# A number of fixed point rounds for each block in a graph dilation

## The chip, the cores and the metric

The kernel runs on one core of a Trainium2 chip. The metric is the device time of one execution in microseconds (us). Five engines work side by side, each with its own queue: TensorE (PE in the profile; PEld is its loading of weights), VectorE (DVE), ScalarE (ACT), GpSimd (POOL) and SyncE (SP), which here only issues transfers.

## The reference

Sixteen graphs of 1024 nodes go through four graph layers with residuals and normalizations between them. The adjacency matrices are symmetric, with about 64 neighbours in a row. The second layer first thins the graph ("dilation"), row by row, and this is the part that matters here:

```
def step(carry, n):                       # n = 0 .. 1023, in order
    row = carry[n]
    num = sum(row)
    sf = (num + 1) // 2 if num > 10 else 1
    rank = cumsum(row)
    rm = row & (rank % sf == 0)           # the middle neighbour, and the last one where num is even
    rm = rm where mask[n] != 0 and num > 1
    carry[n] = row & ~rm
    carry[:, n] = carry[:, n] & ~rm       # the same edges, seen from the other side
```

Each row takes away one or two of its edges, and since the matrix stays symmetric, what an early row takes away changes the counts and ranks of the rows after it.

## The kernel before

The kernel has two paths. `fast_kernel` computes everything under assumptions that it checks on the way. If one fails, a flag that it leaves behind is not zero, and `general_kernel`, a slower path that assumes nothing of the kind, is run after it.

The stages of the fast path follow each other: the first layer (to some 650 us), the dilation (some 650 to 1025 us), the three steps of the second layer, and layers three and four together. The dilation works on all sixteen graphs, whose patterns stay on chip as 8-bit matrices (`Y`, called `carry` in the profile). It goes through eight blocks of 128 rows (`k`), each in two groups of eight graphs (`g`): sixteen steps. A step has three parts.

- `prepare` (L1048) counts, with 64 small matmuls for each half group, the neighbours of each row and their ranks within the block (`sk`, `l1`).
- `fixed_point` (L1080) finds which edges inside the diagonal 128x128 square are removed. Every row's removal depends on how many edges the rows above it removed, so it starts from a guess (`ti`, the count if nothing were removed) and repeats a round: the threshold is made odd (`thr`, L1092), the entries whose rank meets it are marked (`mid`, L1097, 128x1024 elements), eight matmuls with a single column each add the marks of the rows above (`pd`, L1100), and the new guess is their sum with the start value (L1104). In the last two blocks each round also handles the last neighbour of a row (`even`, L1095, and eight more matmuls, L1102). The number of rounds was the constant `EVALS`. After the rounds L1107 compares the last two guesses, and an inequality goes into `bad`, which ends in the flag. The marks are taken out of the square (L1113), and the constants `negc`, `posc` and `wid` for the removals are worked out (L1117 to L1130).
- `removal` (L1133), once for each of the eight graphs, takes the block's edges out of the whole rows: ranks by eight matmuls (L1142, L1144), two ScalarE operations (`q`, L1145), a comparison with `wid` on VectorE (`keep`, L1148), an and (L1149), nine transposing matmuls (`pc`, L1152 to L1156), and a last ScalarE operation that writes the columns (L1157).

In the loop over steps the fixed point of step i is written turn by turn beside the removals of step i-1, and these in turn beside the preparation of step i+1. The first fixed point has no removals beside it; it runs beside the end of the first layer (`after`). The last removals have no fixed point beside them. A program then puts the instructions of each engine in a fixed order from this, and each engine follows its queue. The buffers in this stage: two each of `q`, `keep`, `mid`, `sk`, of the PSUM tile `s` and of the PSUM tile `pc`; one `pd`.

Of the kernel before, what the change touches and what calls it, by code (L numbers as in the profile page):

```python
# [24 lines left out]
BIG = 2.0 ** 53  # L25
LN_EPS = 1e-5
BN_EPS = 1e-5
EVALS = 6
GB = 8
QB = 4  # L30

# [608 lines left out]
def fast_kernel(ctx: ExitStack, tc: tile.TileContext, t: dict, out: bass.AP, flag: bass.AP):  # L640
# [394 lines left out]
    with ExitStack() as ph:  # L1035
# [6 lines left out]
        def words(v):  # L1042
            return v.bitcast(I32)

        def per_member(v):
            return v[:, :, None].to_broadcast([P, v.shape[1], P])
# [33 lines left out]
        def fixed_point(st, k, g):  # L1080

            ks = slice(k * P, (k + 1) * P)
            gs = slice(g * GB, (g + 1) * GB)
            st.negc = negc = tiny.tile([P, GB], F32, name="negc")
            st.wid = wid = tiny.tile([P, GB], F32, name="wid")
            v1m, l1 = st.v1m, st.l1
            nc.vector.tensor_scalar(v1m, l1, 0.5, -0.5, op0=OP.mult, op1=OP.add)
            ti = tiny.tile([P, GB], I32, name="ti")
            nc.vector.tensor_copy(ti, v1m)
            for e in range(EVALS):  # L1090
                thr = tiny.tile([P, GB], I32, name="thr")
                nc.vector.tensor_scalar(thr, ti, 1, None, op0=OP.bitwise_or)  # L1092
                if st.with_last:
                    even = tiny.tile([P, GB], BF16, name="even")
                    nc.vector.tensor_tensor(even, thr, ti, op=OP.is_equal)  # L1095
                mid = sb.tile([P, GB, P], FP8, name="mid")
                nc.vector.tensor_tensor(mid, st.sk, per_member(thr), op=OP.is_equal, saturate=False)  # L1097
                pd = ps_d.tile([P, GB], F32, name="pd")
                for i in range(GB):
                    nc.tensor.matmul(pd[:, i:i + 1], mid[:, i, :], onec, start=True, stop=not st.with_last)  # L1100
                    if st.with_last:
                        nc.tensor.matmul(pd[:, i:i + 1], st.last[:, i, :], even[:, i:i + 1], start=False, stop=True)  # L1102
                tn = tiny.tile([P, GB], I32, name="ti")
                nc.vector.tensor_tensor(tn, pd, v1m, op=OP.add)  # L1104
                prev, ti = ti, tn
                yield
            nc.vector.tensor_tensor(bad[:, 0, k, gs], ti, prev, op=OP.not_equal)  # L1107
            if st.with_last:
                nc.vector.tensor_tensor(st.last, st.last, per_member(even), op=OP.mult, saturate=False)
                nc.vector.tensor_tensor(words(mid), words(mid), words(st.last), op=OP.bitwise_or)  # L1110
            for q in range(GB // QB):
                yw = words(Yq[g * GB // QB + q][:, :, k, ks])
                nc.vector.tensor_tensor(yw, yw, words(mid[:, q * QB:(q + 1) * QB]), op=OP.bitwise_xor)  # L1113


            v = tiny.tile([P, GB], F32, name="v")
            nc.vector.tensor_sub(v, l1, ti)  # L1117
            hw = tiny.tile([P, GB], F32, name="hw")
            nc.vector.tensor_tensor(hw, thr, prev, op=OP.is_equal)
            nc.vector.tensor_sub(negc, hw, v)  # L1120
            nc.vector.scalar_tensor_tensor(hw, v, 0.5, hw, op0=OP.mult, op1=OP.mult)
            nc.vector.tensor_sub(negc, negc, hw)
            st.posc = posc = tiny.tile([P, GB], F32, name="posc")
            nc.vector.scalar_tensor_tensor(posc, v, 2.0, negc, op0=OP.mult, op1=OP.add)
            en = tiny.tile([P, GB], F32, name="en")
            mk = mok[:, g * GB * NT + k:(g + 1) * GB * NT:NT]
            nc.vector.scalar_tensor_tensor(en, v, 10.5, mk, op0=OP.is_gt, op1=OP.mult)
            nc.vector.tensor_tensor(bad[:, 1, k, gs], en, mk, op=OP.not_equal)
            nc.vector.scalar_tensor_tensor(hw, hw, 1.0, en, op0=OP.add, op1=OP.mult)
            nc.vector.tensor_scalar(wid, hw, -1.0, None, op0=OP.add)  # L1130
            yield
# [40 lines left out]
        G2 = B // GB  # L1172
        steps = [(Batch(), k, g) for k in range(NT) for g in range(G2)]
        in_rounds([chain(*(prepare(*s) for s in steps[:G2]), fixed_point(*steps[0])), after(state[B - 1], B - 1)])
        ending.close()
        ps_c = ph.enter_context(tc.tile_pool(name="dl_pc", bufs=2, space=PSUM, reuse_waits="tile"))
# [13 lines left out]
        for i in range(1, len(steps) + 1):  # L1190
            streams = [fixed_point(*steps[i])] if i < len(steps) else []
            streams.append(removals(steps[i - 1], steps[i - 1 + G2] if i - 1 + G2 < len(steps) else None))
            take_turns(streams)
# [672 lines left out]
```

## Time and profile before

| what | us |
|---|---|
| median of three runs (lowest, highest) | 2735.02 (2731.83, 2736.03) |
| the profiled execution | 2734.11 |
| its span | 2732.4 |
| first round of the dilation starts (L1089) | 649.5 |
| first `q` of the removals | 672.4 |
| last L1157 of the dilation ends | 1024.9 |

The profile is a record of one execution. A busy share counts the time in which an engine has an instruction under way. Successive VectorE operations overlap a little: an operation of 1.22 us holds the engine some 1.14 us. "Idle before" is the time for which an engine had nothing under way ahead of an instruction, with the instruction on another engine that ended the wait. In the timeline each line has its start, its duration, the engine and line, what it writes and reads, and the shapes.

From the first `q` of one step to that of the next, the steps of the dilation take (us): 21.4, 22.1, 21.1, 21.0, 21.0, 20.9, 20.9, 20.9, 20.9, 20.9, 21.6, 23.4, 28.0, 22.7, 24.7.

### The profile page before, as it was taken

The numbers are of one execution on the slowest core, as the hardware profiler recorded it, in microseconds if no ns is written. First come the engines' busy times: TensorE is split into PE (matmuls) and PEld (weight loads), VectorE is DVE, ScalarE is ACT, GpSimd is POOL, SyncE is SP. The second block draws the span as 40 slices with busy tenths as digits, with TensorE's granted clock in tenths as the row PEclk, the third lists the DMA queues.
The fourth block names the chain that finished last, engine by engine and source line by source line (L and its number), as shares of the span: only waits on it lengthen the run. The fifth ranks groups of instructions, "written<-read, shape, count | busy, mean of one in ns | idle before, by whom it ended". The sixth has DMA issues, their size and how long they took to land.

```text
span 2732.4 us, 41821 instructions
## 1 busy us (share of the span) xinstructions
PE 2552.2 (93%) x15048; PEld 1688.8 (62%) x15048; DVE 2108.6 (77%) x5650; ACT 1977.0 (72%) x3188; POOL 317.1 (12%) x287
## 2 busy tenths in 40 slices
PE   7999999994899888998999998999999999999986
PEld 3444444442666657887778887456666666666655
DVE  5887778875999986776678877577787787787785
ACT  6888889873888786666655543777777777777773
POOL 0000000003000001121112123001010010001001
PEclk9999999996999999999999999999999999999998
DMA  5455445430000042233356655101222211111100
GB/s 189 162 169 171 165 167 177 157 114 23 2 2 2 2 183 96 94 108 124 132 203 224 254 205 211 39 24 62 70 77 73 90 62 62 62 62 62 46 24 25
DMA packets 120810, 285.38 MB, mean 104 GB/s; under 512 B 12305, under 2 KB 65425, under 8 KB 113425
## 3 DMA queue, kind: packets, MB, share of 16 engines
q1 hardware_dynamic: 101280, 203.33, 22.4%
q0 software_dynamic: 19312, 79.28, 7.5%
q8 instruction: 121, 1.98, 0.3%
q14 instruction: 97, 0.79, 0.1%
HBM read 202.72 MB, written 79.82 MB: 103 GB/s over the span
## 4 chain that ended last, share of the span: by engine, by line
PE 62%; DVE 16%; issue 9%; POOL 5%; ACT 4%; DMA 3%; SPq 0%; POOLq 0%; ACTq 0%; DVEq 0%
PE acc L974 8%; PE ph L1618 8%; PE pmm L724 8%; PE acc L1678 7%; PE ph L766 6%; PE acc L1306 5%; PE ph L759 4%; PE pmm L1690 3%; POOL rn L745 2%; PE ph L1605 2%; PE ph L1432 2%; DVE mid L1097 2%; POOL ln_rstd L745 1%; PE s L1144 1%; DVE keep L1148 1%
## 5 line engine op out<-in xcount | busy, mean ns | idle before, releaser
L745 POOL TENSOR_TENSOR ln_rstd<-ln_rstd,mhalf 128x8 f32<-128x8 f32 (+1 forms) x68 | 108.3, 1592 | 1347.6 <-DVE ln_rstd L742 879.7
L974 PE MATMUL acc<-em,hs 128*128 128x512 f32 x512 | 260.1, 607 | 1.9 <-DVE past L1075 1.3
L724 PE MATMUL pmm<-xT,G 128*128 128x512 f32 x512 | 261.8, 604 | 0.0
L1678 PE MATMUL acc<-ex,hs 128*128 128x512 f32 x512 | 248.9, 596 | 7.4 <-DVE hs L1705 4.5
L801 ACT ACTIVATE xn<-xn,ln_nb,ln_rstd 128x128 f32<-128x128 f32 x512 | 204.6, 481 | 70.3 <-DVE ln_nb L799 70.3
L1306 PE MATMUL acc<-a,lo 128*128 128x512 f32 x768 | 240.4, 398 | 15.3 <-DVE lo L1273 15.3
L1306 PE MATMUL acc<-a,hi 128*128 128x512 f32 x768 | 241.4, 399 | 3.8 <-ACT hi L1272 3.6
L986 ACT ACTIVATE em<-em,mx 128x1024 f32<-128x1024 f32 x128 | 146.4, 1144 | 63.5 <-DVE mx L984 63.0
L1698 ACT ACTIVATE ex<-em,mn 128x1024 f32<-128x1024 f32 x128 | 146.8, 1147 | 44.6 <-DVE mn L1695 43.9
L984 DVE CUSTOM_DVE_ANT_0 em<-pmm,msk 128x1024 f32<-128x1024 f32 x128 | 156.0, 1219 | 27.0 <-PE pmm L724 26.4
L1306 PEld LDWEIGHTS acc<-a,lo 128*128 128x128 f32 x768 | 144.3, 190 | 52.2 <-DVE lo L1273 22.6
L1690 PE MATMUL pmm<-G,hT 128*128 128x512 f32 (+3 forms) x416 | 175.3, 523 | 0.1
L1695 DVE CUSTOM_DVE_ANT_0 em<-pmm,msk 128x1024 f32<-128x1024 f32 x128 | 155.3, 1214 | 24.4 <-PE pmm L1692 22.3
L1306 PEld LDWEIGHTS acc<-a,hi 128*128 128x128 f32 x768 | 144.1, 191 | 34.1 <-ACT hi L1272 4.6
L1157 ACT ACTIVATE carry<-pc,negone 128x1024 fp8e4<-128x1024 f32 x128 | 140.8, 1114 | 27.0 <-PE pc L1156 21.7
L932 ACT ACTIVATE carry<-an 128x1024 fp8e4<-128x1024 f32 x128 | 134.4, 1050 | 21.7 <-DMA an<-in_adj 20.7
L981 ACT ACTIVATE msk<-carry,l0nbig 128x1024 bf16<-128x1024 fp8e4 x128 | 145.4, 1137 | 0.0
L1618 PE MATMUL ph<-A,hi 128*128 128x512 f32 x512 | 143.1, 420 | 1.2 <-DVE zn L1607 0.7
L1686 ACT ACTIVATE msk<-A,nbig 128x1024 bf16<-128x1024 fp8e4 x128 | 144.1, 1136 | 0.0
L1678 PEld LDWEIGHTS acc<-ex,hs 128*128 128x128 f32 x512 | 88.7, 190 | 76.8 <-issue 54.6
L1295 ACT CAST a<-A 128x1024 fp32r<-128x1024 fp8e4 x96 | 99.1, 1050 | 50.9 <-PE acc L1306 50.9
L1295 ACT CAST a<-carry 128x1024 fp32r<-128x1024 fp8e4 x96 | 99.3, 1049 | 47.6 <-PE acc L1306 47.4
(319 smaller groups left out, 6237.4 us busy)
## 6 DMA issues: line engine op xcount, KB each, us to landing
an<-in_adj SPq DMA_DIRECT2D x128, 512.0 KB, 3.6
adj_d<-carry POOLq DMA_DIRECT2D x16, 1024.0 KB, 4.2
A<-dil_d SPq DMA_DIRECT2D x16, 1024.0 KB, 5.6
rdeg<-rdeg_d SPq DMA_DIRECT2D x32, 512.0 KB, 3.8
A<-adj_d SPq DMA_DIRECT2D x16, 1024.0 KB, 4.8
ag_d<-ag POOLq DMA_DIRECT2D x24, 512.0 KB, 5.0
ag<-ag_d SPq DMA_DIRECT2D x24, 512.0 KB, 5.0
xn<-in_x SPq DMA_DIRECT2D x16, 512.0 KB, 4.3
```

The lines of the kernel that those rows point to most:

```text
L724: nc.tensor.matmul(p[:, h * 512:(h + 1) * 512], lhsT, rhs[:, h * 512:(h + 1) * 512], start=True, stop=True)
L745: nc.gpsimd.tensor_tensor(r, r, mhalf[:, :n], op=OP.pow)
L766: nc.tensor.matmul(p, W, x[:, c], start=(i == 0), stop=(i == len(pairs) - 1))
L801: nc.scalar.activation(r[:, k.start + i, :], r[:, k.start + i, :], AF.Identity, scale=rstd[:, i:i + 1], bias=nb[:, i:i + 1])
L974: nc.tensor.matmul(s.acc[:, c], hs, em[:, c], start=(jt == 0), stop=(jt == NT - 1))
L984: nc.vector.tensor_tensor_reduce(em, e, msk, 1.0, 3.0e38, op0=OP.add, op1=OP.min, accum_out=mn)
L1295: nc.scalar.copy(a, A[:, 2 * i:2 * i + 2, c])
L1306: nc.tensor.matmul(acc, part[:, jt, :], pieces[h * NT // 2 + i][:, j, :], start=(jt == 0 and p == 0), stop=(jt == NT - 1 and p == 1))
L1618: nc.tensor.matmul(p, part[:, jt, :], A[jt][:, c], start=(jt == 0 and i == 0), stop=(jt == NT - 1 and i == 1))
L1678: nc.tensor.matmul(s.acc[:, c], hs, ex[:, c], start=(jt == 0), stop=(jt == NT - 1))
L1690: nc.tensor.matmul(e[:, c], s.hT[:, js], s.G[:, c], start=True, stop=True)
L1695: nc.vector.tensor_tensor_reduce(row, e, msk, 1.0, 0.0, op0=OP.add, op1=OP.min, accum_out=mn)
```

## The change

The constant becomes a tuple with an entry for each block, and the loop takes the entry of its block. The comparison of the last two guesses and the flag stay, so a block that isn't settled after its rounds still sends the whole computation through the general path.

```
-EVALS = 6
+EVALS = 2, 3, 4, 7, 7, 3, 3, 9
...
             nc.vector.tensor_copy(ti, v1m)
-            for e in range(EVALS):
+            for e in range(EVALS[k]):
                 thr = tiny.tile([P, GB], I32, name="thr")
                 nc.vector.tensor_scalar(thr, ti, 1, None, op0=OP.bitwise_or)
```

Blocks 0, 1, 2, 5 and 6 get fewer rounds, blocks 3, 4 and 7 more.

## The prediction

> **What bounds the kernel now.** I read the page's engine shares first. TensorE is busy 93% of the span, but the change touches only one stage, so what it is worth has to be read there. The stage was found with the groups by line (L1097, the comparison inside the loop that changes, runs only between 649 and 1002 us), and then cut into stretches.
>
> ```profile
> span 2732.4 us, 41821 instructions
> PE 2552.2 (93%) x15048; PEld 1688.8 (62%) x15048; DVE 2108.6 (77%) x5650; ACT 1977.0 (72%) x3188; POOL 317.1 (12%) x287
> ```
>
> The view of busy time by stretches. The first is the fixed point of the first block alone, the next three are single steps of the steady part, the fifth is the step with the last fixed point, the sixth is the last removals alone:
>
> ```profile
> 649.00:672.00 23.00, 10.82 (x147) 7.54 (x146) 20.14 (x73) 3.36 (x9) 1.64 (x1) 0.50 0.03 10
> 737.00:758.00 21.00, 18.95 (x254) 13.46 (x251) 20.13 (x58) 18.23 (x25) 0.00 (x0) 1.00 0.01 2
> 758.00:779.00 21.00, 19.00 (x254) 13.61 (x251) 20.11 (x57) 18.24 (x26) 0.00 (x0) 1.00 0.01 2
> 779.00:800.00 21.00, 19.03 (x254) 13.62 (x252) 20.10 (x57) 18.27 (x26) 0.00 (x0) 1.00 0.01 2
> 979.30:1004.00 24.70, 18.19 (x255) 13.46 (x255) 23.24 (x65) 19.19 (x26) 3.77 (x7) 1.00 0.65 262
> 1004.00:1022.00 18.00, 15.27 (x153) 10.77 (x151) 9.48 (x20) 17.62 (x25) 0.53 (x1) 0.91 0.72 288
> ```
>
> After the length come TensorE, its weight loads, VectorE, ScalarE and GpSimd. In a steady step VectorE is busy 20.1 of 21.0 us, ScalarE 18.2; in the last row ScalarE is busy 17.6 of 18.0 and VectorE only half. So VectorE sets the steady step, and ScalarE is the next floor.
>
> What VectorE does in three steady steps (groups by line, 737 to 800 us; count, busy us, mean ns, idle before):
>
> ```profile
> L1097 DVE TENSOR_TENSOR mid<-sk,thr 128x1024 fp8e4<-128x1024 f16 x18 | 22.0, 1220 | 0.2
> L1148 DVE TENSOR_SCALAR keep<-q,wid 128x1024 fp8e4<-128x1024 f16 x24 | 17.9, 746 | 0.0
> L1149 DVE TENSOR_TENSOR carry<-carry,keep 128x256 int32<-128x256 int32 x24 | 10.1, 419 | 0.0
> L1092 DVE TENSOR_SCALAR thr<-ti 128x8 int32<-128x8 int32 x18 | 3.0, 168 | 0.2
> ```
>
> Six comparisons, eight keeps and eight ands per step; almost no idle time before any of them. Last, the timeline of VectorE at the first fixed point and in the removals that nothing accompanies:
>
> ```profile
> 655.48 1.21 DVE L1097 TENSOR_TENSOR mid<-sk,thr 128x1024 fp8e4<-128x1024 f16 x1
> 656.62 0.15 DVE L1075 TENSOR_TENSOR past<-l,s 128x4 f32<-128x4 f32 x1
> ...
> 661.47 1.21 DVE L1097 TENSOR_TENSOR mid<-sk,thr 128x1024 fp8e4<-128x1024 f16 x1
> ...
> 663.69 1.21 DVE L1097 TENSOR_TENSOR mid<-sk,thr 128x1024 fp8e4<-128x1024 f16 x1
> ...
> 671.43 0.16 DVE L1130 TENSOR_SCALAR wid<-hw 128x8 f32<-128x8 f32 x1
> ...
> 1014.52 0.75 DVE L1148 TENSOR_SCALAR keep<-q,wid 128x1024 fp8e4<-128x1024 f16 x1 [0.90 <-ACT q L1145]
> ...
> 1016.69 0.75 DVE L1148 TENSOR_SCALAR keep<-q,wid 128x1024 fp8e4<-128x1024 f16 x1 [0.88 <-ACT q L1145]
> ```
>
> Two things to see. A lone round costs 663.69 - 661.47 = 2.22 us (compare, eight small matmuls, add, or), though VectorE works only some 1.3 us of it. And removals alone come every 16.69 - 14.52 = 2.17 us, with VectorE waiting for ScalarE: 8 x 2.17 = 17.4 us is ScalarE's floor for a step.
>
> [...] In the steady rows weight loads are 13.6 of 21.0 us (65%), so TensorE's 90% is not taken as the bound. [...] with the `ti` add late, VectorE idles with later keeps queued behind. So the order of the instructions matters, and I read it from the changed program as built.
>
> **The change part by part.** Rounds per step (each block is two steps, one per group of eight batches): -4, -3, -2, +1, +1, -3, -3, +3 for blocks 0 to 7; in all 96 become 76. Outside this stage the order on TensorE, VectorE, ScalarE and GpSimd is unchanged; on SP one load moves by a few places. I call period i the time from the first q (L1145) of removals i-1 to that of removals i; fixed point i runs inside it. The price of a removed round on VectorE, start to next start where nothing waits: compare 1.14, add 0.10, or 0.08, together 1.32 us; with `even` (blocks 6, 7) 1.41.
>
> *Start (step 0, block 0).* This fixed point runs alone and the first removal waits for its end. In the new order the second comparison, at 655.48, is the last. After it come the add at 657.29, two xors (0.2 each), some ten small operations (0.08), and the tail of layer 0's last batch that used to lie between the rounds: two r (0.6 each), xn (1.14), two statistics (0.2). That gives `wid` at about 661.3 and the first q at 661.5 instead of 672.4: -10.9. TensorE's clock is 0.50 there before and stays so.
>
> *Period 1 (block 0, second group, -4).* Before 21.4. ScalarE's eight normalizations (L801, 3.2 us), which used to end just before the first q, now stand inside this period: 17.4 + 3.2 = 20.6, so -0.8. VectorE's sum is 5.3 lower and hidden.
>
> *Periods 2 to 5, 10, 11 (blocks 1, 2, 5).* Before 22.1, 21.1, 21.0, 21.0, 20.9, 21.6: 127.7. VectorE alone would take 20.95 - 3 x 1.32 = 17.0, or 18.3 with two rounds less; ScalarE needs 17.4. Two engines that are both nearly full don't interlock perfectly. Lower bound: the larger of the two, 4 x 17.4 + 2 x 18.3. Upper bound: in the new order three or four rounds, four keeps and the tail stand ahead of `wid` (I add up 10.9 us of VectorE, against 8.7 of ScalarE), then four removals at ScalarE's pace (8.7); with no lead carried between the halves 19.6. q has two buffers, so half the surplus should be carried: 18.4 for three rounds, 18.9 for four. 4 x 18.4 + 2 x 18.9 = 111.4: -16.3.
>
> *Periods 12, 13 (block 6, -3 each).* Before 23.4 and 28.0, well above ScalarE's floor, so the full VectorE price: -6 x 1.41 = -8.5.
>
> *Periods 6 to 9 (blocks 3, 4, +1 each).* VectorE is full: +4 x 1.32 = +5.3.
>
> *Periods 14, 15 (block 7, +3 each).* Lower bound 1.41 a round if removals fill every gap; upper 2.9, the slow rounds there now (2.88 to 2.96 in period 15). In the new order the eight removals of period 14 are used up before the last two rounds, and those stand alone (2.56 is the shortest round in this block); in period 15 the last one does. I take 2.1: 6 x 2.1 = +12.6. The last removals (20.9) start later by that and are otherwise the same.
>
> Sum: -10.9 - 0.8 - 16.3 - 8.5 + 5.3 + 12.6 = -18.6. Later layers keep their order and shift. Against the profiled execution's 2734.11: 2715.5. The median of the three runs is 2735.0, inside their spread of 4 us, so I leave it.
>
> **Rivals.** (A) *Poor interlock.* The cut steps reach only 19.6, and block 6 gains 6.0 instead of 8.5: the sum becomes -10.9 - 0.8 - 10.1 - 6.0 + 5.3 + 12.6 = -9.9, 2724. For it: in-order queues, removals bunched behind `wid`. Against it: two buffers of q, keep and pc. (B) *Good interlock.* Cut steps at their floor (-21.7) and added rounds at 1.41 (+8.5): -28, 2706. (C) *Slower.* The rounds removed were hidden behind TensorE's in-order queue and give back only their slots there (eight matmuls, 0.3 us), while the added ones lengthen the path to `wid`, which releases the next removals, by whole round trips: 4 x 2.07 + 6 x 2.9 = 25.7. With 26 rounds removed after the start: -10.9 - 26 x 0.3 + 25.7 = +7, 2741. It decides if a removed round yields under (25.7 - 10.9) / 26 = 0.57 us. For it: TensorE 19 of 21 us busy. Against it: VectorE's lack of idle time, and weight loads at 65%. (D) *The flag.* If a block isn't settled, L1107 sets `bad` and the general path runs after all this. It isn't in this trace; its row loop alone has 127 x 8 x 9 chained small VectorE operations, at 0.16 us some 1.5 ms more. Following the fixed point on the inputs of seed 0, the most rounds that any batch needs, with the one that confirms it, are 1, 1, 3, 5, 5, 2, 1, 5, nowhere more than the change allows.
>
> **How the numbers follow.** Forecast 0.78, A 0.13, B 0.04, C 0.04, D 0.01. The forecast's own bounds are 2706 (both unknowns at their low ends) and 2724; A's upper side reaches 2729 with added rounds at 2.9. For 8 in 10 I take 2705 to 2726. Within 0.2% (5.5 us, about what this measurement can tell) lies only A's tail: 0.03. Slower: C and D, 0.05. Faster: 0.92.
>
> **What would show it.** 76 comparisons at L1097, 1.22 us each; first q near 661.5; periods near 20.6, then 18.4 to 18.9, 22.3 in blocks 3 and 4, 18.4 in block 5, some 21.4 in block 6, and 27 to 31 in block 7; the last relu (L1157) of the stage near 1006 instead of 1024.9; everything after it as before. Wrong would be cut steps that stay near 21 (C), VectorE still without idle time there, or lines of the general path.

## The result, and the profile after

The changed kernel takes 2726.12 us (median of nine runs, 2721.38 to 2730.35), the kernel before 2733.41 us beside it (nine runs). The ratio is 0.9976, with a 95% interval of 0.9966 to 0.9986: faster by 7.3 us, where 18.6 were forecast. The profiled execution took 2724.04 us against 2734.11, 10.1 less; some 3 us of that difference are scatter between executions.

The page of the kernel after, engine shares:

```profile
span 2722.3 us, 41453 instructions
PE 2544.4 (93%) x14888; PEld 1682.1 (62%) x14888; DVE 2083.0 (77%) x5590; ACT 1977.7 (73%) x3188; POOL 317.0 (12%) x287
```

VectorE has some 26 us less to do, and the span is only 10 us shorter. Where the rest stayed is seen in the stage. This table compares the first `q` (L1145) of one step with that of the next, from the timelines; "cut steps" are periods 2 to 5, 10 and 11, added up (after: 21.0, 20.0, 20.6, 20.5, 18.1 and 20.3 us).

| us | before | forecast | after |
|---|---|---|---|
| first `q` | 672.4 | -10.9 | 661.7 (-10.7) |
| period 1 | 21.4 | -0.8 | 23.3 (+1.9) |
| cut steps | 127.7 | -16.3 | 120.5 (-7.2) |
| periods 6 to 9 (+1 round each) | 83.7 | +5.3 | 89.2 (+5.5) |
| periods 12, 13 (-3 rounds each) | 51.4 | -8.5 | 44.3 (-7.1) |
| periods 14, 15 (+3 rounds each) | 47.4 | +12.6 | 61.3 (+13.9) |
| the last removals | 21.0 | 0 | 22.6 (+1.6) |
| last L1157 of the stage ends | 1024.9 | -18.6 | 1023.0 (-1.9) |
| profiled execution | 2734.11 | -18.6 | 2724.04 (-10.1) |

So the stage itself gained 1.9 us, not 18.6, and 8.2 us came after it. The view of busy time by stretches of the kernel after: the first fixed point and what follows, a cut step, a step with a seventh round, a step with nine rounds (columns as before: length, TensorE, weight loads, VectorE, ScalarE, GpSimd, TensorE's clock, and last the DMA share and GB/s):

```profile
651.00:672.00 21.00, 15.20 (x172) 10.65 (x169) 18.19 (x73) 8.98 (x17) 2.73 (x2) 0.63 0.04 11
706.00:726.00 20.00, 17.61 (x227) 12.79 (x226) 16.24 (x49) 18.06 (x25) 0.00 (x0) 1.00 0.01 2
787.10:811.10 24.00, 21.29 (x293) 15.46 (x291) 23.41 (x66) 20.25 (x26) 0.00 (x0) 1.00 0.01 2
939.10:971.60 32.50, 23.38 (x357) 17.80 (x356) 29.88 (x83) 19.49 (x26) 0.00 (x0) 0.88 0.01 2
```

In the cut step (second line) VectorE's busy time did fall, from 20.1 to 16.2 us, yet the step takes 20.0 instead of 21.0. No engine is full: ScalarE, which was to be the floor at 17.4, is busy 18.1 us and stands still for 1.9. The view of waits over two cut steps, 706 to 747 us (total, times, longest), says for what:

```profile
DVE keep L1148 <- ACT q L1145: 6.2, 5, 2.9
...
ACT carry L1157 <- PE pc L1156: 2.8, 6, 0.7
PE s L1144 <- ACT q L1145: 2.4, 5, 0.8
...
PE s L1142 <- ACT q L1145: 1.2, 2, 0.6
```

VectorE waits for ScalarE, ScalarE for TensorE, and TensorE for ScalarE, until it has read a PSUM tile `s` that the next ranks are to be written to. One turn in the timeline of the same kernel, the three engines together:

```profile
706.68 0.70 ACT L1145 ACTIVATE q<-s,posc 128x512 f16<-128x512 f32 x1
...
707.47 0.69 DVE L1071 TENSOR_TENSOR sk<-s,uY 128x512 f16<-128x512 f32 x1 [0.99 <-PE s L1069]
...
708.14 0.74 DVE L1148 TENSOR_SCALAR keep<-q,wid 128x1024 fp8e4<-128x1024 f16 x1
708.25 0.72 ACT L1145 ACTIVATE q<-s,negc 128x512 f16<-128x512 f32 x1
...
708.82 0.73 ACT L1145 ACTIVATE q<-s,posc 128x512 f16<-128x512 f32 x1
...
708.94 0.42 DVE L1149 TENSOR_TENSOR carry<-carry,keep 128x256 int32<-128x256 int32 x1
709.02 0.65 PE L1144 MATMUL s<-step,carry 128*128 128x512 bf16 x3 [0.49 <-ACT q L1145]
...
709.51 0.22 PE L1152 MATMUL pc<-carry,identb 128*128 128x128 fp8e4 x1
...
709.62 0.55 PE L1156 MATMUL pc<-identb,carry 128*128 128x128 bf16 x7
...
710.21 1.11 ACT L1157 ACTIVATE carry<-pc,negone 128x1024 fp8e4<-128x1024 f32 x1 [0.66 <-PE pc L1156]
```

TensorE stands for 0.49 us, since both `s` tiles are taken until the `q` of 708.25 has read one. ScalarE is through with its second `q` at 709.55 and then stands for 0.66 us, until the transposes `pc` of the removal before are there. In TensorE's queue these stand behind the ranks that waited for `s`, and I took that for the reason; the times say otherwise. They read what VectorE's `and` (L1149) writes, it ended at 709.36, and they began at 709.51. Over the 16 removals of these two steps they began 0.05 to 0.36 us after the end of their own `and`, 0.10 on average. So the ranks held them back by some 0.1 us here, and the rest of ScalarE's wait runs over VectorE. The `q` of that removal had ended at 707.38, but its `keep` (708.14) stood behind `sk` (L1071), which had waited 0.99 us for the preparation's matmuls, and two small operations stood between `keep` and `and`.

The kernel before has such waits too, behind a full VectorE (737 to 800 us, three steps):

```profile
ACT q L1145 <- PE pc L1156: 3.6, 3, 1.2
ACT carry L1157 <- PE pc L1156: 2.9, 3, 1.0
...
PE s L1142 <- ACT q L1145: 1.8, 3, 0.6
...
PE s L1144 <- ACT q L1145: 0.8, 3, 0.3
```

At this point the waits over `s` were a suspicion; the experiments below went through other explanations first.

What came after the stage starts at its seam, where the next stage begins. The timelines of VectorE and TensorE there, before:

```profile
1031.65 0.27 DVE L1400 TENSOR_REDUCE nodeg<-d 8x1 f32<-8x128 f16 x1 [6.93 <-DMA d<-row]
...
1032.97 1.15 DVE L1273 TENSOR_TENSOR lo<-n,hi 128x1024 fp32r<-128x1024 f32 x1
...
1034.17 1.22 PE L1306 MATMUL acc<-a,lo 128*128 128x512 f32 x2 [2.93 <-DVE lo L1273]
...
1043.95 0.49 PE L1432 MATMUL ph<-Wx,hT 128*128 128x128 f32 x2
```

and after:

```profile
1026.26 1.23 DVE L1273 TENSOR_TENSOR lo<-n,hi 128x1024 fp32r<-128x1024 f32 x1 [4.07 <-ACT hi L1272]
1027.41 0.27 DVE L1400 TENSOR_REDUCE nodeg<-d 8x1 f32<-8x128 f16 x1
...
1027.54 1.22 PE L1306 MATMUL acc<-a,lo 128*128 128x512 f32 x2
...
1037.52 0.49 PE L1432 MATMUL ph<-Wx,hT 128*128 128x128 f32 x2
```

Before, `lo` (L1273) was queued behind L1400, which waited 6.93 us for a load, and TensorE waited for `lo`, 2.93 us; the `hi` that `lo` reads had ended at 1029.12. In the new order `lo` stands first. The first L1432 comes 1043.95 - 1037.52 = 6.4 us earlier, 4.5 more than the stage gave. I had taken the order outside the stage as unchanged; at this one place it isn't. The load was shorter too: from issue to landing it took 5.1 us before and 1.6 after. With it and the old order, `lo` would have stood at some 1027.5 us (an estimate: 1026.22, where the load landed, and the 1.32 us from L1400 to `lo` before), so either of the two gives most of the 4.5 us.

### The profile page after: what moved, and what is told of

It reads as the page before. It is cut to its first block, busy times and chain, and to the rows that moved or that the text cites. A ratio compares the mean times of both kernels' runs of the same rounds, so it can differ in the third digit from the quotient of the medians.

```text
span 2722.3 us, 41453 instructions
## 1 busy us (share of the span) xinstructions
PE 2544.4 (93%) x14888; PEld 1682.1 (62%) x14888; DVE 2083.0 (77%) x5590; ACT 1977.7 (73%) x3188; POOL 317.0 (12%) x287
## 4 chain that ended last, share of the span: by engine, by line
PE 47%; DVE 18%; issue 8%; POOL 5%; ACT 4%; DMA 2%; POOLq 0%; DVEq 0%; ACTq 0%
PE ph L1618 8%; PE acc L1678 7%; PE ph L766 5%; PE acc L1306 4%; PE ph L759 3%; PE pmm L1690 3%; PE ph L1432 3%; PE acc L974 2%; PE pmm L724 2%; PE ph L1605 2%; DVE mid L1097 2%; POOL rn L745 2%; DVE keep L1148 2%; POOL ln_rstd L745 1%; ACT q L1145 1%
## 5 line engine op out<-in xcount | busy, mean ns | idle before, releaser
L984 DVE CUSTOM_DVE_ANT_0 em<-pmm,msk 128x1024 f32<-128x1024 f32 x128 | 156.1, 1220 | 22.8 <-PE pmm L724 21.9
L1157 ACT ACTIVATE carry<-pc,negone 128x1024 fp8e4<-128x1024 f32 x128 | 141.4, 1116 | 27.3 <-PE pc L1156 24.5
L724 PEld LDWEIGHTS pmm<-xT,G 128*128 128x128 f32 x512 | 87.3, 190 | 73.8 <-issue 73.8
```

The lines of the kernel that those rows point to most:

```text
L724: nc.tensor.matmul(p[:, h * 512:(h + 1) * 512], lhsT, rhs[:, h * 512:(h + 1) * 512], start=True, stop=True)
L984: nc.vector.tensor_tensor_reduce(em, e, msk, 1.0, 3.0e38, op0=OP.add, op1=OP.min, accum_out=mn)
```

## Experiments

The letters in the expectations: F, the cut steps have a floor near 20 us, however few rounds they have; V, a round costs VectorE's 1.32 to 1.41 us both ways; T, the floor comes from TensorE's queue and the number of the preparation's matmuls in it; Q, from the two buffers of `q`; B, from rounds bunched at the head of a step; L, from the chain over preparation and fixed point; O, from the two `s` tiles. All diffs are against the changed kernel.

**1 to 3. Cuts alone, additions alone, fewer still.**

```
e1_cuts:   EVALS = 2, 3, 4, 6, 6, 3, 3, 6
e2_adds:   EVALS = 6, 6, 6, 7, 7, 6, 6, 9
e3_needed: EVALS = 1, 1, 3, 5, 5, 2, 1, 5
```

> Only the cuts (2, 3, 4, 6, 6, 3, 3, 6). Theory F (a removed round frees VectorE, but a step that is cut meets a practical floor near 20 us, set by ScalarE's operations and their in-order waits, whatever the number of rounds below five): the stage keeps what the changed kernel showed in its cut steps, and loses nothing in blocks 3, 4 and 7: last L1157 some 21 us earlier than before, about 25 us less in all with the 4 us of the seam to the next stage, 2708 to 2711. Rival V (a round costs its 1.3 us of VectorE everywhere, and the changed kernel fell short because of its longer steps and their neighbours): 36 us or more less, under 2700.

> Only the additions (6, 6, 6, 7, 7, 6, 6, 9). Theory F: VectorE is full in blocks 3 and 4 (+1.3 a round), and in block 7 the added rounds stand alone at 2.3 each: the stage 19 us longer than before, 4 us given back at the seam, about 2748. Rival V: 1.3 to 1.4 a round throughout, the stage 14 us longer, about 2743.

> The rounds that these inputs need and no more (1, 1, 3, 5, 5, 2, 1, 5). Theory F: periods of blocks 0, 1, 2, 5 near 20 us, no shorter than with two or three rounds; blocks 3 and 4 near 20.5; block 7 one round shorter each; the start 2 to 5 us shorter still: the stage 32 to 38 us shorter than before, about 2695. Rival V: periods fall to ScalarE's 17.4 us, the stage 52 us shorter or more, about 2680.

The cuts alone took 2707.6 us, ratio 0.9912 (0.9898 to 0.9925). Their cut steps add up to 121.6 us, as in the changed kernel (120.5), so it isn't the added rounds that spoil them. The additions alone took 2742.05 us, ratio 1.0039 (1.0026 to 1.0053); in the stage they cost 14.1 us. With the fewest rounds that this input needs the time was 2696.86 us, ratio 0.9873 (0.9858 to 0.9888), with no round to spare for other inputs. Its cut steps still take 121.2 us together, though they have 1, 3 and 2 rounds instead of 3, 4 and 3. So the floor of F holds, and V falls for removed rounds. For added rounds it is the other way round: 14.1 us in the stage is V's number, and F's 19 falls. F's totals for e1_cuts and e3_needed came true in part by luck: their stages ended 18.8 and 27.6 us earlier, less than the 21 and 32 to 38 expected, and the rest came after the stage.

**4. One round everywhere.**

```
-EVALS = 2, 3, 4, 7, 7, 3, 3, 9
+EVALS = 1, 1, 1, 1, 1, 1, 1, 1
-            nc.vector.tensor_tensor(bad[:, 0, k, gs], ti, prev, op=OP.not_equal)
+            nc.vector.tensor_tensor(bad[:, 0, k, gs], ti, ti, op=OP.not_equal)
```

> One round in every block, with the check comparing the last guess with itself, so that the marks of blocks 2, 3, 4, 5 and 7 are not settled and the check of convergence is left out. It shows a step's floor. Theory F: steady periods of 19.5 to 20 us. Rival V: 17.4 to 18 us, ScalarE's pace in removals alone.

A single execution took 2686.25 us; periods 2 to 15 have a mean of 20.2 us (18.6 to 21.8). (All runs with one round, and e11_sixtwice, are single executions.) Stretch and waits (782 to 845 us, three steps) of this run:

```profile
803.00:823.50 20.50, 17.79 (x210) 12.78 (x208) 14.01 (x43) 18.17 (x25) 0.00 (x0) 1.00 0.01 2
```

```profile
DVE keep L1148 <- ACT q L1145: 11.7, 11, 2.7
DVE sk L1071 <- PE s L1069: 6.4, 7, 0.9
ACT carry L1157 <- PE pc L1156: 4.5, 10, 0.7
...
PE s L1069 <- DVE past L1075: 3.1, 6, 0.6
...
PE s L1142 <- ACT q L1145: 2.2, 5, 0.8
...
ACT q L1145 <- PE s L1142: 1.5, 7, 0.2
PE s L1144 <- ACT q L1145: 1.0, 3, 0.5
```

VectorE is busy 14 of 20.5 us. Its busy time is surely not the bound, and the period is what it was. The rounds are nearly free here; something else makes the 20 us.

**5 to 7. Fewer matmuls in the preparation, rounds spread out, a third `q`.**

```
e5_fewer, on top of e4_one:
-                    for kb in range(NT):
+                    for kb in ((k, NT - 1) if k < NT - 1 else (0, k)) if k else range(NT):
     (and the first of these kb starts the sum)
e6_spaced:
-                yield
+                for _ in range(max(1, 9 // EVALS[k]) if (k, g) != (0, 0) else 1):
+                    yield
e7_q3:
-            q = sb.tile([P, N], F16, name="q")
+            q = sb.tile([P, N], F16, name="q", bufs=3)
     (and one buffer instead of two for mid and last)
```

> One round in every block as in e4_one, and after block 0 the preparation counts over two of the eight row blocks only: 16 matmuls a step in place of 64, everything that reads the counts kept; the counts of the other blocks are left out. Theory T (the floor near 20.5 us comes from TensorE's queue: the preparation's 64 matmuls stand ahead of the ranks that ScalarE waits for): periods fall to 17.5 to 18.5 us. Rival Q (the floor comes from the two buffers of q and keep and the order in which the removals stand): periods stay near 20.

> The changed kernel's rounds, with extra turns between them, so that in blocks 1, 2, 5 and 6 the end of the fixed point (wid) stands behind five or six of the eight removals instead of three or four. Theory B (bunching: the removals left behind wid go at ScalarE's pace while VectorE is idle): cut periods of 18.5 to 19.5 us, the whole 8 to 12 us shorter than the changed kernel, about 2716. Theory T: no better than 1 us a period, within 5 us of the changed kernel's 2726.

> The changed kernel's rounds with three buffers of q (one of mid and of last, to make room). Rival Q: ScalarE can run one removal further ahead, cut periods fall to 18.5 to 19.5 us and the whole to about 2716. Theory T: cut periods stay within 0.7 us of the changed kernel's, the whole within 5 us of 2726.

Spread rounds took 2721.74 us, ratio 0.9959 (0.9944 to 0.9974), with 118.2 us for the cut steps: B falls. The third `q` took 2724.91, ratio 0.997 (0.9959 to 0.9981), with 121.0 us: Q falls, as far as this run can tell, since the single `mid` could take back what the third `q` gives. In e5_fewer the late steps took 17.5 us:

```profile
722.20:741.10 18.90, 16.32 (x184) 11.84 (x184) 17.74 (x63) 17.84 (x26) 0.00 (x0) 1.00 0.01 2
...
854.40:871.90 17.50, 14.02 (x138) 9.92 (x136) 10.22 (x23) 17.49 (x25) 0.00 (x0) 1.00 0.01 1
```

I first read that as proof of T, and it was none. In the second line VectorE has 23 instructions where a step with a round and a preparation has some 42: nothing but removals is left there. With so few row blocks read, a preparation no longer waits for the removals before it; preparations and fixed points ran ahead, two to a step (first line), and were over by 820 us. (It then went through the general path: 11137 us in all, which puts that rival's price at some 8.5 ms.)

**8. The start alone.**

```
+EVALS = 2, 6, 6, 6, 6, 6, 6, 6
```

> Only block 0 cut (2, 6, 6, 6, 6, 6, 6, 6), with the instructions at the seam in the order of before. The first q comes 10.7 us earlier, period 1 gives back 2 us, all else is as before and the seam gives nothing: 8 to 9 us in all, 2724 to 2726. If the 4 us that the changed kernel gained at the seam came from the earlier end of the stage and not from the order there, they show here too, and it is 2720 or less.

It took 2719.25 us, ratio 0.9954 (0.994 to 0.9968): 13.2 us less, and less time than the whole change. The first `q` came 10.4 us earlier and the stage ended 6.5 us earlier; the other 7 us came after the stage, with the old order at the seam. By the expectation's own test (2720 or less) that would put the seam's gain down to the earlier end of the stage, but the trace doesn't bear this out: the first L1432 comes 7.8 us earlier than before, so 1.3 us were gained at the seam, where the load took 3.7 us instead of 5.1, and the rest came later. I return to that at the end.

**9 to 11. The number of the preparation's matmuls, with its waits kept.**

```
e9_third, on top of e4_one:
-                    for kb in range(NT):
+                    kbs = sorted({k - 1, k, NT - 1}) if k else range(NT)
+                    for kb in kbs:
     (and kbs[0] starts the sum; both comparisons behind the flag as in the text)
e10_twice, on top of e4_one, and e11_sixtwice, with six rounds:
-                    for kb in range(NT):
+                    for kb in [*range(NT)] * 2:
```

> One round everywhere, and after block 0 the preparation of a step issues 24 matmuls instead of 64: of the row blocks it keeps the last one before its own (the one that the latest removals wrote), its own, and the last. So a preparation still waits for the same removals as before, which it did not in the run with 16 matmuls. Left out: the counts over the other row blocks, and both comparisons behind the flag compare a value with itself, so ranks and output are not the reference's. Theory T (TensorE's in-order queue, in which the preparation's matmuls stand among the removals' ranks, sets the floor of 20 to 20.5 us): 40 matmuls fewer at some 0.05 us each are 2.0 us a step, so periods of 18 to 18.7 us. Rival L (the length of the chain from the removals over the preparation and the fixed point to the next removals sets it, not the number of matmuls): periods stay at 20 to 20.5.

> One round everywhere, the round's comparison behind the flag compares a value with itself (left out: a test that the rounds sufficed, and the rounds themselves), and every preparation issues its 64 matmuls twice over, the second pass overwriting the first with the same sums. VectorE and ScalarE do exactly the work of the run with one round. Theory T: 64 matmuls more at some 0.05 us each are 3.2 us a step, so periods of 22.5 to 24 us instead of 20 to 20.5. Rival L (a chain of waits, with TensorE holding slack): periods under 21.

> Six rounds everywhere as in the kernel before, and every preparation issues its 64 matmuls twice over, to the same sums. If VectorE alone bounds the step with six rounds (20.1 us busy of 21.0), the doubled matmuls are hidden: periods of 21 to 21.5 us. If TensorE's queue bounds that step as well (theory T carried to six rounds): 3.2 us more, periods of 23.5 to 24.5 us. In between would say that the two engines share the bound.

A preparation is 64 matmuls a step, 32 for each half group (not 64 for each, as the section on the kernel has it). With 24 instead of 64 the mean of periods 2 to 15 went from 20.2 to 19.8 us, and periods 2 to 10 took 19.4 or 19.5 each. With 128 the mean was 21.5. With six rounds and 128 it was 23.1, against 22.2 before. So 40 matmuls fewer give 0.4 of the 2.0 us that T asked for, and 64 more cost 1.0 to 1.3 of 3.2: T carries a part and not the floor, and L, for which nothing should have moved, isn't it either. (The runs with 24 matmuls, e9_third, e13_third_s3 and e17_third_s3b, went through the general path as well, 11162, 11234 and 11138 us in all, so only their steps are compared.) What remains shows in the waits of e9_third (740.5 to 798.8 us, three steps; its lines from 1070 on stand one later):

```profile
DVE keep L1149 <- ACT q L1146: 14.6, 15, 2.5
...
PE s L1145 <- ACT q L1146: 5.1, 6, 0.9
PE s L1143 <- ACT q L1146: 4.6, 6, 0.9
...
ACT carry L1158 <- PE pc L1157: 3.3, 6, 0.6
ACT q L1146 <- PE s L1143: 1.5, 7, 0.2
```

TensorE, busy 15.8 of the 19.4 us, stands 3.2 us a step for an `s` tile, and ScalarE 1.6 us a step for TensorE; ScalarE is busy 17.9 us of the step. From this came theory O.

**12 to 15. A third `s` tile, `pd` in its ring.**

```
-        ps_d = ph.enter_context(tc.tile_pool(name="dl_pd", bufs=1, ...
-        ps_s = ph.enter_context(tc.tile_pool(name="dl_ps", bufs=2, ...
+        ps_s = ph.enter_context(tc.tile_pool(name="dl_ps", bufs=3, ...
...
-                pd = ps_d.tile([P, GB], F32, name="pd")
+                pd = ps_s.tile([P, GB], F32, name="pd", tag="s")
```

> One round everywhere, all 64 matmuls of the preparation (left out: the further rounds, and the test behind the flag that they sufficed), and the PSUM tile s of the ranks gets three buffers instead of two; pd, which had a bank of its own, takes one of the three in turn. Theory O (the steps' floor is the two queues' fixed order: TensorE's next ranks wait for an s tile that ScalarE has not yet freed, the transposes pc for ScalarE's next operation stand behind them in TensorE's queue, so both engines stand still in turn): periods fall from a mean of 20.2 us to 18 to 19. Theory T (the number of the preparation's matmuls): 19.8 to 20.5, as before. Rival L (the chain over preparation and fixed point): the same, 19.8 to 20.5.

> The run with one round and 24 matmuls in a preparation, with the third s tile beside it (it leaves out the same as that run: counts over the other row blocks, the further rounds, the tests behind the flag). There the period was 19.4 us with TensorE busy 15.8 and VectorE 13.9. Theory O: 17.4 to 18.3 us, ScalarE's own pace. Theory L or T: 19.0 to 19.5, unchanged.

> The changed kernel's rounds (2, 3, 4, 7, 7, 3, 3, 9) with three s tiles, pd among them; nothing left out. Theory O: the cut steps (periods 2 to 5, 10, 11) fall from 20.2 us to 18.5 to 19.3, seven or so us in all, and the time from 2726 to 2715 to 2720. Theory T or L: periods as before, 2724 to 2728. A risk for both: each round's pd now takes its turn among the s tiles, which can make steps of seven and nine rounds longer.

> Rounds 2, 3, 4, 6, 6, 3, 3, 6 with three s tiles, pd among them; nothing left out. With two s tiles this took 2707.6 us. Theory O: 2697 to 2702. Theory T or L: 2705 to 2710.

Neither theory's numbers: one round took 2745.3 us with periods near 24 (24.0 with 24 matmuls too), the changed kernel's rounds 2769.87 (ratio 1.0132, 1.0114 to 1.0149), e1's rounds 2759.03 (1.0085, 1.0061 to 1.0108). The timeline of TensorE in e12_s3:

```profile
804.45 0.50 PE L1069 MATMUL s<-step,carry 128*128 128x128 bf16 x3 [1.18 <-DVE past L1075]
806.21 0.38 PE L1100 MATMUL pd<-onec,mid 128*128 128x1 bf16 x8 [1.25 <-DVE mid L1097]
806.44 1.23 PE L1144 MATMUL s<-step,carry 128*128 128x512 bf16 x4
```

`pd` takes its turn in the ring of the `s` tiles, the ranks are queued behind the round that fills it, and TensorE waits for VectorE. Its granted clock is lower too, 0.83 from 800 to 820 us, where the cut step shown first has 1.00. The four rank matmuls of 806.44 take 1.23 us; in the kernel before four took 1.25 us at a granted clock of 0.50 (667.54 us), and in that cut step four take 0.70 us (707.29 us). This edit changed two things and could not decide.

**16 to 18. A third `s` tile, `pd` in the preparation's single tile.** As before, but for

```
+                pd = ps_b.tile([P, GB], F32, name="pd", tag="s0")
```

> One round everywhere, 64 matmuls in a preparation (left out: the further rounds and the test behind the flag that they sufficed), three s tiles, and pd takes its turn in the single bank of the preparation's s instead of among the ranks' tiles, where it held the next ranks back for 1.2 us at a time. Theory O (TensorE and ScalarE stand still in turn over two s tiles): periods of 18 to 19 us instead of a mean of 20.2. Rival L (a chain that does not run over the s tiles) or T: 19.8 to 20.5.

> The same with 24 matmuls in a preparation (left out besides: the counts over the other row blocks, and both tests behind the flag). With two s tiles the period was 19.4 us, with TensorE standing 3.2 us a step for an s tile and ScalarE 1.6 for TensorE. Theory O: 17.4 to 18.3. Rival L or T: 19.0 to 19.5.

> Rounds 2, 3, 4, 6, 6, 3, 3, 6, three s tiles, pd in the preparation's bank; nothing left out. With two s tiles and a bank for pd this took 2707.6 us. Theory O with rounds that seldom meet the preparation: 2697 to 2703. Where each round must wait for the preparation's bank, which it holds some 3 us twice a step: 2712 or more. Rival L or T: 2705 to 2710.

With one round the time was 2668.07 us against 2686.25, periods 2 to 9 have a mean of 18.0 us, and periods 2 to 15 of 18.6 against 20.2. Two of them, and the same kernel's waits over three steps (755.7 to 809.8 us):

```profile
773.70:791.70 18.00, 17.23 (x210) 12.82 (x210) 13.71 (x42) 17.63 (x25) 0.00 (x0) 1.00 0.00 1
791.70:809.80 18.10, 17.38 (x209) 12.88 (x209) 13.70 (x42) 17.73 (x26) 0.00 (x0) 1.00 0.01 2
```

```profile
DVE sk L1071 <- PE s L1069: 1.1, 3, 0.4
...
PE s L1142 <- ACT q L1145: 0.6, 3, 0.3
ACT carry L1157 <- PE pc L1156: 0.4, 2, 0.2
```

TensorE's wait for `s` went from 3.2 us (L1142 and L1144 in e4_one) to 0.6, ScalarE's for `pc` from 4.5 to 0.4, and ScalarE is busy 17.6 of 18.0 us with all 64 matmuls in the preparation. With 24 the steps take 17.4 and 18.0 in turn. O's numbers hold. One link of its circle doesn't: in e4_one the transposes began 0.05 to 0.24 us after the end of their `and` (mean 0.09), here 0.05 to 0.18 (mean 0.09), so at most some 0.2 us each of standing behind the ranks was there to be gained, and on average nothing was. What fell are the waits: TensorE's for `s`, ScalarE's for the ranks (1.5 us on L1142 and 0.6 on L1144 to none) and for `pc`, and VectorE's for the preparation's matmuls (`sk`, 6.4 us to 1.1), behind which `keep` and `and` stand. With e1's rounds, nothing left out, the time was 2698.83 us, ratio 0.988 (0.9864 to 0.9897), against 2707.6 with two `s` tiles; its cut steps add up to 110.5 us. Two of them:

```profile
702.50:720.20 17.70, 16.57 (x224) 12.20 (x221) 16.38 (x49) 17.56 (x26) 0.00 (x0) 1.00 0.01 2
720.20:738.30 18.10, 16.49 (x217) 11.95 (x217) 16.72 (x50) 16.61 (x25) 0.00 (x0) 1.00 0.01 2
```

The order of the instructions is made anew for each of these kernels, so the tile and the order that follows from it were changed together, and `pd` was moved with them. Neither another order alone nor `pd` moved alone, with two `s` tiles, was tried, so which of these waits sets the floor stays open. `pd` in the preparation's tile has a price too: the six-round steps, periods 6 to 9, take 86.9 us against e1's 84.9.

## Why the prediction was wrong

**The step that failed: periods 2 to 5, 10 and 11, -16.3 forecast and -7.2 measured.** The removed comparisons left VectorE as forecast, and ScalarE is then the busiest of the two, as forecast. Wrong was its floor of 17.4 us with half of a surplus carried over in "two buffers of q". The 17.4 came from the last removals, where neither TensorE nor VectorE has anything else in its queue. Beside a preparation and rounds, the three engines wait for each other: TensorE for one of the two `s` tiles (3.6 us over two cut steps), which the prediction left out where it named buffers, ScalarE for ranks and `pc` (0.6 and 2.8 us), and `pc` for a `keep` and an `and` that stand behind other work on VectorE. A cut step took 20.1 us on average, not 18.4 to 18.9. Three runs carry this: one round with VectorE 6 us below the period leaves it near 20, a third `q` leaves it too, and a third `s` tile, with the order that goes with it, brings the cut steps to 110.5 us, where the sum of the prediction had 111.4.

**Period 1 (-0.8, measured +1.9):** 17.4 + 3.2 was the sum, and it missed by 2.7 us, about as much as a cut step of 120.5 / 6 = 20.1 us lies above 17.4. The same cause isn't shown for it: with the third `s` tile it takes 22.8 instead of 25.9 with one round, but 23.2 instead of 24.1 with e1's rounds.

**The start (-10.9)** held, -10.7, and e8_start shows it by itself at -10.4.

**The added rounds** held: +5.5 for +5.3 in blocks 3 and 4, and 2.3 us a round for 2.1 in block 7. In e2_adds, without the cuts, the same rounds of block 7 took 1.8 us each. Two rounds stood alone in period 15 where I had one; the last removals then took 1.6 us more, which I had at nothing. VectorE's price held where rounds were added in blocks 3 and 4 and failed where they were removed, since removing them made other waits the bound.

**Block 6 (-8.5)** measured -7.1: near, and its second step, which fell from 28.0 to 21.1, ended close to the cut steps.

**"Later layers keep their order and shift", at 0,** was wrong twice: the seam gave 4.5 us, by the order there and a shorter load, and another 3.7 us came later. Of the 7.3 us that the medians differ by, the stage has 1.9.

**The rivals.** A, the poor interlock, had the right kind of mistake in mind, with cut steps of 19.6. The waiting in order that it counted on shows in the kernel before: a `keep` ended at 961.09 us, and VectorE then stood 0.94 us for the `pd` of the next `ti` (962.03), with the `and` of that `keep` (962.12) queued behind it. That its 2724 met the profiled execution is chance, as its sum ends with the stage, at -9.9 where -1.9 was measured. C's mechanism, that removed rounds had lain beside other work, is true of a cut step for the rounds below the floor: 16 of them gave 7.2 us, 0.45 each, under the 0.57 where C was to decide. The kernel still became faster because the start gave its 10.7 us, and because the ten added rounds cost 19.4 us in place of C's 25.7; most of what is left of the gain came after the stage, where C had nothing. That weight loads at 65% speak against TensorE as the bound was the prediction's estimate; what the runs show is that with 64 matmuls more a step of six rounds took 23.1 us in place of 22.2 (e11_sixtwice). D didn't occur.

Two sums of the prediction are slightly off and change nothing here: B's cut steps at their floor are 127.7 - 106.2 = 21.5, not 21.7, and the forecast with both unknowns at their upper ends (cut steps of 19.6, added rounds at 2.9) is 2726.5, not 2724.

## What to carry to other kernels

When the fullest engine was relieved here, the next floor was not the busy sum of the next engine (ScalarE, 18.1 us) but that sum with waits that it already had (20.0 us); read those waits, and follow each to the operation that really came last, before taking the sum. Here ScalarE's waits for `pc` (6.5 us over three steps) and TensorE's for `s` (2.6 us) stood in the profile before the change, under a VectorE that was busy 20.1 of 21.0 us. The engine that a wait names needn't be the cause: ScalarE's wait was named after TensorE, which began 0.10 us on average after VectorE's result. A pace measured where an engine has the others to itself, ScalarE's 17.4 us here, was a lower bound and not a price: a cut step took 20.1. And an experiment that takes work away may take a wait with it: count the instructions of the stretch before believing it.

## What the runs showed besides

TensorE's granted clock in the second layer is not the same from kernel to kernel, though the engines' order there is the same. Over the five stretches of 100 us from 1250 to 1750 us its means are 0.98, 0.97, 1.00, 0.98, 0.91 before and 0.98, 1.00, 1.00, 1.00, 0.93 after; in e8_start 1.00, 0.98, 1.00, 1.00, 0.95. If the clock is 0.50 where it isn't 1.00, as in the first stretch of the prediction, that is an estimated 32, 18 and 14 us at half clock. The kernel after is 6.4 us ahead at the seam and about 10 at 1750 us, e8_start about 8 and then about 18 (its profiled execution is the fastest of its five, 2.6 us under their median). It is not these two alone: in the profiled executions of all fourteen further kernels that kept to the fast path, between 1 and 12 us came after the stage. The clock also differs between executions of one kernel: the nine of the changed kernel have means of 0.975 to 0.980. And e12_s3 had 0.83 from 780 to 840 us, with TensorE busy 48.8 of the 60 us, where the changed kernel had 1.00 from 706 to 747 us, with TensorE busy 35.3 of the 41. What sets the clock isn't shown by these runs. Whether the earlier start changed it in e8_start wasn't tried by itself and stays open, and so does how much of the last 3.7 us belongs to the change.
